# When the extra work of a causal attention is issued: turns and narrow products in steps of their own, queries and keys in VectorE's banks, a shorter first load, the last sends after the attention

## The chip, the cores and the metric

The kernel runs on one core of a Trainium2 chip. The metric is the device time of one execution in microseconds (us). A core has five engines that work side by side, each through a queue of its own: TensorE (PE), VectorE (DVE), ScalarE (ACT), GpSimd (POOL) and SyncE (SP, which here issues most DMAs). Matmul results land in PSUM[...]. The clock at which TensorE runs varies with time, and the profile shows what was granted as a share of full speed.

## The reference

The input x has 16 sequences of 512 rows with 128 channels, float32. Two transformer blocks follow one another, cut here to what matters:

```python
x = x + attn0(layernorm(x)) @ w_proj.T + b_proj   # causal, 16 heads of 8, qkv with bias
x = x + moe(layernorm(x))      # 8 experts 128->512->128, exact gelu, top 2 by softmax
x = x + attn1(layernorm(x))    # not causal, 16 heads of 8, no output projection
x = x + ffn(layernorm(x))      # silu(gate) * up, 352 wide, operands rounded to FP4 blocks
```

The change lies in the first attention and in what runs beside it: the gate of the mixture of experts (logits, the two best experts, the place of each row in its expert's list) and the sending of the normalised rows to those places in DRAM.

## The kernel before, in words

**Groups and steps.** A sequence's 16 heads are taken in four groups (`G = 4`) of two pairs of strips, and a group's keys in four blocks of 128 (`NC = 4`). One *step* is one group with one key block, so a sequence is 16 steps and the first attention 256. The loop at L1015 issues, step by step, what TensorE does: row maxima (`row_max`, tile ps_max) for the group three ahead (`LEAD = 3`), scores (`score`, ps_sc), and the value products of the step before (`attend`, ps_av, put off through the list `behind`). In the first two steps of a group a maximum and a score are each issued in two parts, in the order maximum, score, extra work, maximum, score; in the last two steps there is one of each. In the third step of a group the sums of the group before are turned and divided (`divide`, ps_d, L840).

**How the maxima get into the scores.** After every second group `part_max` splits the maxima in two halves (DVE), `put_max` turns them (ps_mx) and writes them as rows mT into the strips q by DMA (L777), where the next scores need them.

**Extra work.** All else hangs on four dictionaries with a step's number as key. `soon` runs at the head of the step, `ahead` and `later` between the first and the second parts, `last_of` at the end (L1039 to L1059). The extra work of a sequence consists of three lists:

- *The prologue* of a coming sequence b (`prologue`, L639), which starts at position 8 (of 0 to 15) of the sequence two before and takes positions 12 to 17 for its turn, queries, keys, values, spreads and bias: layer norm (`stats`, `moments` with a power on POOL at L203, `scale` with the normalised xn by ACT at L214), the turn of xn (ps_t), the products for queries and keys (`split`, ps_qk, with a rounded half hi by ACT at L656 and the remainder lo by DVE at L669), their writes to DRAM (L678) and DMAs that spread them over the strips, eight and one more for each half (`first` and `second`, L687), the values (ps_v) and the output bias added to x by POOL (`biased`, L713).
- *The end* of a finished sequence: position 3 of the next one turns the result (`turn_back`, aT), position 4 multiplies it by w_proj (`finish`, ps_o).
- *The gate* (`gate_after`, L991), with offsets counted from position 4: norm of the new x (xg by ACT at L214), its turn, the logits (`logits`, ps_g, four matmuls of 8 columns), and in every second sequence `choices`: seven pieces of DVE work, among them the ranks (`place`, ps_n), and then 16 `send`s, one per step, each an indirect DMA issued by POOL (L520). For the last two sequences the gate runs by single sequence and has eight sends. `clear_steps` (L363) fills with zeros what no row will be sent to: `rest`, and eight `region`s, on SP's queue.

**What is in order.** `in_order` (L152) chains every matmul and turn in the order in which the program issues them, and so most of POOL's work. `Lane` (L167) does the same for every DVE instruction of the first attention that goes through `vec`. ACT's order and SP's come from the scheduler, by the program's order and what it estimates. The waits on data are added to this.

**PSUM.** Tiles from `for_dve` take one of two pairs of banks (pool ps_s): ps_max, ps_d, ps_o, ps_g, ps_n, and in general what DVE reads. Tiles from `for_act` take one of four single banks in turn (pool ps_c): ps_sc, ps_av, ps_t, ps_mx, ps_v and, before, ps_qk.

**Start.** L76 to L84 load the constants and all 16 sequences (256 KB each) on SP's queue; bqk's columns `bp` follow (L591). The prologues of sequences 0 and 1 and the maxima of the first three groups run ahead of the loop. `strips` (L618) and `value_columns` (L628) fill the constant parts of the strips and of the values.

**End.** After the loop the remaining sequences are finished, and what is left in `later` is issued in the order of steps (L1075): the gate of the last sequence and its sends, and the plan of the experts' tiles. Then the mixture of experts loads its first tile of rows.

The lines at which the extra work of a step is issued:

```python
if maxima:
    maxima.pop(0)()
scores.pop(0)()
if now in ahead:
    ahead.pop(now)()
...
for f in later.pop(now, []):
    f()
for f in maxima + scores:
    f()
if now in last_of:
    last_of.pop(now)()
```

## Time and profile before

| what | before |
| --- | --- |
| runs, us | 2481.8, 2484.9, 2493.6 (median 2484.9) |
| profiled execution: time of its own, and span | 2462.05, 2460.2 us |
| mean granted clock of TensorE | 0.922 |
| instructions | 38583 |
| start, to the first score of the loop | 0 to 62.7 us |
| first attention, to the end of the loop | 62.7 to 926.3 us |
| one sequence of it, mean of numbers 1 to 13 (least, most) | 54.27 (48.96, 58.92) us |
| first turns of the mixture of experts | 972.3 us |
| second attention, about | 1290 to 2100 us |

Times inside the trace count from the start of the span. The profiled execution is one of its own, and it need not have the time of the runs' median: here it is 22.9 us shorter. In the profile's engine table, the columns are busy time, share of the span and number of instructions; PEld are TensorE's weight loads, which overlap its matmuls. In the slices, each digit is a fortieth of the span in tenths of full load, and PEclk is the granted clock. In the list of stretches, the row gives from and to, the length, the busy time with the number of instructions for PE, PEld, DVE, ACT and POOL, the clock, the mean load of the DMA engines and GB/s. In the timeline, a row gives the start, the length, the engine, line, operation and tiles, how many such instructions, and in brackets what the engine waited for just before. Nearly all matmuls and turns carry the lines of the helpers, L264 and L267, so tiles tell them apart.

### The profile page before, as it was taken

The numbers are of one execution on the slowest core, as the hardware profiler recorded it, in microseconds if no ns is written. First come the engines' busy times: TensorE is split into PE (matmuls) and PEld (weight loads), VectorE is DVE, ScalarE is ACT, GpSimd is POOL, SyncE is SP. The second block draws the span as 40 slices with busy tenths as digits, with TensorE's granted clock in tenths as the row PEclk, the third lists the DMA queues.
The fourth block names the chain that finished last, engine by engine and source line by source line (L and its number), as shares of the span: only waits on it lengthen the run. The fifth ranks groups of instructions, "written<-read, shape, count | busy, mean of one in ns | idle before, by whom it ended". The sixth has DMA issues, their size and how long they took to land.

```text
span 2460.2 us, 38583 instructions
## 1 busy us (share of the span) xinstructions
PE 2138.1 (87%) x13324; PEld 1067.2 (43%) x13324; DVE 1710.3 (70%) x3106; ACT 1389.1 (56%) x2716; POOL 891.4 (36%) x1384
## 2 busy tenths in 40 slices
PE   5999999999999973989998899999899999957776
PEld 2444444444444431656665333333333333335454
DVE  5666666666666636956435788888788888488887
ACT  1565655555565541332334777777777777844443
POOL 4334453545454444032002333322333321054453
PEclk7999998899898975999999999999999999978888
DMA  6112222222122292445552222322232221000000
GB/s 185 54 56 64 62 73 66 88 80 70 60 67 65 62 125 66 140 139 161 158 150 66 63 90 75 85 63 64 63 91 75 83 63 54 2 5 13 18 18 17
DMA packets 156929, 184.47 MB, mean 75 GB/s; under 512 B 25647, under 2 KB 120976, under 8 KB 148544
## 3 DMA queue, kind: packets, MB, share of 16 engines
q1 hardware_dynamic: 147806, 164.55, 23.9%
q0 software_dynamic: 8352, 17.20, 2.5%
q8 instruction: 107, 1.75, 0.3%
q14 instruction: 86, 0.70, 0.1%
q10 hardware_dynamic: 578, 0.26, 0.1%
HBM read 116.55 MB, written 63.28 MB: 73 GB/s over the span
## 4 chain that ended last, share of the span: by engine, by line
PE 38%; DVE 14%; ACT 4%; POOL 3%; issue 2%; DMA 1%; POOLq 0%; ACTq 0%; DVEq 0%
PE ps_av L264 10%; PE ps_max L264 7%; PE ps_h L264 5%; PE ps_sc L264 5%; PE ps_y L264 5%; DVE mx L751 4%; ACT pt L804 3%; PE ps_gu L264 2%; DVE q_t L1123 1%; PE ps_qk L264 1%; DVE q_t L1124 1%; POOL xn L250 1%; DVE q_m L1115 1%; POOL q_v L1112 1%; PE ps_t L267 1%
## 5 line engine op out<-in xcount | busy, mean ns | idle before, releaser
L751 DVE TENSOR_REDUCE mx<-ps_max 128x2 f32<-128x1024 f32 (+1 forms) x896 | 1014.8, 1147 | 385.0 <-PE ps_max L264 373.9
L804 ACT ACTIVATE pt<-ps_sc 128x512 f32<-128x512 f32 (+2 forms) x1792 | 900.8, 568 | 474.7 <-PE ps_sc L264 447.0
L264 PE MATMUL ps_av<-pt,va 128*32 128x512 f32 (+3 forms) x4096 | 498.6, 553 | 19.8 <-POOL pt L809 14.4
L264 PE MATMUL ps_sc<-q,k 64*128 64x512 f32 (+3 forms) x2048 | 461.5, 413 | 30.2 <-ACT pt L804 24.6
L264 PE MATMUL ps_max<-k,q 64*128 64x512 f32 (+3 forms) x2048 | 437.7, 445 | 31.9 <-DVE mx L751 31.5
L809 POOL TENSOR_SCALAR_AFFINE_SELECT pt<-pt 128x128 f32<-128x128 f32 (+1 forms) x768 | 249.6, 332 | 437.2 <-ACT pt L804 421.1
L264 PEld LDWEIGHTS ps_max<-k,q 64*128 64x128 f32 x2048 | 190.2, 193 | 459.3 <-issue 164.4
L264 PEld LDWEIGHTS ps_sc<-q,k 64*128 64x128 f32 x2048 | 220.6, 191 | 161.8 <-ACT pt L804 85.7
L1242 ACT ACTIVATE h<-ps_h,b1t 128x512 f32<-128x512 f32 x156 | 107.1, 687 | 193.6 <-PE ps_h L264 193.5
L264 PE MATMUL ps_y<-w2t,h 128*128 128x128 f32 x1248 | 148.6, 278 | 6.0 <-DVE yt L1256 6.0
L264 PE MATMUL ps_h<-xT,w1t 128*128 128x512 f32 x312 | 150.7, 615 | 3.3 <-DVE xT L275 1.9
L264 PEld LDWEIGHTS ps_av<-pt,va 128*32 128x32 f32 x4096 | 85.7, 110 | 154.2 <-issue 101.2
L264 PEld LDWEIGHTS ps_y<-w2t,h 128*128 128x128 f32 x1248 | 144.4, 194 | 8.6 <-DVE yt L1256 6.4
L1176 POOL DMA_INDIRECT got<-y_rows,backs x128 | 124.1, 970 | 63.0 <-issue 32.5
L520 POOL DMA_INDIRECT x_rows<-xg,slots x128 | 126.2, 986 | 50.8 <-issue 33.5
L264 PE MATMUL ps_max<-mask_bf,ident_bf 128*128 128x128 bf16 (+1 forms) x768 | 130.8, 255 | 0.0
L236 POOL TENSOR_TENSOR ln_rstd<-ln_ve,mhalf 128x4 f32<-128x4 f32 x32 | 34.5, 1079 | 251.2 <-DVE ln_nm L238 248.4
L264 PE MATMUL ps_gu<-wgT,xqT 128*128 128x352 f32 x128 | 67.9, 620 | 63.5 <-DVE hid L1369 35.0
L177 DVE RECIPROCAL rec<-ps_d 128x16 f32<-128x16 f32 x128 | 32.1, 251 | 92.5 <-PE ps_d L267 92.5
L662 POOL TENSOR_TENSOR lo<-full,hi 128x512 fp32r<-128x512 f32 x32 | 41.0, 1282 | 148.3 <-ACT hi L660 148.3
L264 PE MATMUL ps_qk<-xnT,wp 128*128 128x512 f32 x128 | 80.2, 714 | 11.8 <-ACT pt L804 10.4
L835 ACT COPY av_sb<-ps_av 128x512 f32<-128x512 f32 x128 | 75.8, 592 | 16.0 <-PE ps_av L264 11.5
(205 smaller groups left out, 2362.1 us busy)
## 6 DMA issues: line engine op xcount, KB each, us to landing
q<-d SPq DMA_DIRECT2D x256, 128.0 KB
k<-d SPq DMA_DIRECT2D x256, 128.0 KB
d<-hi SPq DMA_DIRECT2D x64, 256.0 KB
d<-lo SPq DMA_DIRECT2D x64, 256.0 KB
xt<-x_rows SPq DMA_DIRECT2D x39, 262.0 KB
w1t<-in_w_dram SPq DMA_DIRECT2D x39, 256.0 KB
w2t<-in_w_dram SPq DMA_DIRECT2D x39, 256.0 KB
y_rows<-yt SPq DMA_DIRECT2D x39, 256.0 KB
```

The costliest lines, as they stand in the source:

```text
L177: ins = f(*args, **kw)
L236: in_order(nc.gpsimd.tensor_tensor(rstd, ve, mhalf, ALU.pow), queue="pool")
L250: ins = (by or nc.gpsimd).tensor_scalar(xn[:, c, 0:E], xb[:, c, :], nm[:, c : c + 1], rstd[:, c : c + 1], ALU.add, ALU.mult,)
L264: return in_order(nc.tensor.matmul(out, lhsT, rhs, start=start, stop=stop))
L520: ins = in_order(nc.gpsimd.indirect_dma_start(out=x_rows[:, :], out_offset=bass.IndirectOffsetOnAxis(ap=slots[:, b0 + u, k, c : c + 1], axis=0
L662: nc.gpsimd.tensor_tensor(lo, full, hi.bitcast(F32), ALU.subtract),
L751: nc.vector.tensor_reduce(hv["mx"][:, c, :, p0 : p0 + m], s4, AX.X, ALU.max),
L804: nc.scalar.activation(pt[:, 0 : m * n], ps[:, 0 : m * n], AF.Exp, scale=SCALE)
L809: nc.gpsimd.affine_select(head, head, pattern=[[0, m], [1, P]], base=0, channel_multiplier=-1, compare_op=ALU.is_ge, fill=0.0,),
L835: nc.scalar.copy(t, acc.pop(0))
L1176: ins = in_order(nc.gpsimd.indirect_dma_start(out=got[:, c, :], out_offset=None, in_=y_rows[0 : min(NT, NE * (b + 1)) * TS, :], in_offset= ...
L1242: nc.scalar.activation(h[:, f, :], ps, AF.Gelu, bias=t["b1"][:, f : f + 1])
```

## The change

It has four parts, all in the first attention; the second attention and everything after are left as they are, and the same instructions are issued, in another order and with other banks.

1. **Steps.** The dictionary `ahead` is no longer used by the first attention. The prologue of sequence b hangs on fixed positions of sequence b - 2: statistics 5 steps before that sequence begins and moments 1 before, xn at its position 3, the bias at 4, its turn at 5, queries and keys together at 7 (their remainders at the end of that step), half of the spreads at 9, the values at 11, the other half 16 steps on. The gate moves too: xg from offset 3 to 4 (position 7 to 8), its turn from 4 to 5 (position 9), the logits in two halves at offsets 6 and 7, the ranks and what follows one step each from offset 8 on.
2. **Banks.** In the first attention, queries and keys share one pair of VectorE's banks in place of two single banks of ScalarE's ring.
3. **Start.** Only two sequences are loaded first; the other 14 loads are issued on SP's queue after the spreads of sequences 0 and 1. The weights' copies move behind the first statistics, and what makes the bias row (a copy, two matmuls, a copy) moves behind the second ones, as `bias_rows`.
4. **End.** The sends of sequence 14 move behind the loop, and the fill `rest` no longer orders the sends.

Offsets in `todo` count from `step`, which is position 4 of the next sequence, and `whens` chooses between the head of the step, its middle and its end. The core of the diff:

```diff
@@ -78,10 +78,13 @@
 
 
     xs = []
-    for b in range(B):
-        xb = cp.tile([P, NC, E], F32, name=f"x{b}")
-        nc.sync.dma_start(out=xb, in_=x_in[b].rearrange("(c p) e -> p c e", p=P))
-        xs.append(xb)
+    xs = [cp.tile([P, NC, E], F32, name=f"x{b}") for b in range(B)]
+
+    def fetch(b):
+        return nc.sync.dma_start(out=xs[b], in_=x_in[b].rearrange("(c p) e -> p c e", p=P))
+
+    for b in range(2):
+        fetch(b)
 
 
     wqkv_sb = cp.tile([E, 3 * E], F32, name="wqkv_sb")
@@ -368,10 +371,11 @@
         def rest():
             vec.tensor_copy(ends_at, free[0:1, :])
             at = NE * CAP + REST
-            nc.sync.dma_start(
+            ins = nc.sync.dma_start(
                 out=rows_of(x_rows, slice(at, at + TS)),
                 in_=zeros.to_broadcast([P, TS // P, ROW]),
             )
+            tc.declare_no_dep(ins.ins, group="sent", reason="other rows")
 
         def region(e):
             at = nc.sync.value_load(
@@ -411,16 +415,22 @@
         def turned(u):
             st["xnT"] = transposed(pool, for_act, st[u], "xnT", nc.scalar.copy)
 
-        def logits(u):
+        def logits(u, part):
             xnT = st["xnT"]
-            if u == 0:
+            if u == 0 and part == 0:
                 st["lg"] = small("g_lg")
-            ps = for_dve("ps_g")[:, 0, 0 : NC * NE]
-            for c in range(NC):
-                mm(ps[:, c * NE : (c + 1) * NE], xnT[:, c * P : (c + 1) * P], wg_sb)
+            if part == 0:
+                st["ps"] = for_dve("ps_g")[:, 0, 0 : NC * NE]
+            for c in range(NC // 2 * part, NC // 2 * (part + 1)):
+                mm(
+                    st["ps"][:, c * NE : (c + 1) * NE], xnT[:, c * P : (c + 1) * P], wg_sb,
+                    start=c == 0, stop=c == NC - 1,
+                )
+
+        def logits_out(u):
             vec.tensor_tensor(
                 st["lg"][:, u * NC : (u + 1) * NC, :],
-                ps.rearrange("p (c e) -> p c e", e=NE),
+                st.pop("ps").rearrange("p (c e) -> p c e", e=NE),
                 bg_bc.to_broadcast([P, NC, NE]),
                 ALU.add,
             )
@@ -511,9 +521,11 @@
                 vec.tensor_copy(to[:, :, E + 2 : E + 3], d[:, at])
                 vec.tensor_copy(to[:, :, E : E + 1], st["r", 1][:, at])
 
+
         choices = [
-            first_of_two, second_of_two, both, place, lambda: (taken(), slot(1)),
-            lambda: (slot(2), shares()), fill,
+            ((0, logits_out), (1, first_of_two)), ((1, second_of_two),), ((1, both),),
+            ((1, place),), ((0, taken), (1, lambda: slot(1))),
+            ((1, lambda: (slot(2), shares())),), ((1, fill),),
         ]
 
         def send(u, k, c):
@@ -531,7 +543,7 @@
             if b0 + u < B - 2:
                 tc.declare_no_dep(ins.ins, group="cleared", reason="other rows")
 
-        return norm, turned, logits, choices, send
+        return norm, turned, logits, logits_out, choices, send
 
 
 
@@ -595,12 +607,14 @@
 
 
...
+            def bias_rows():
...
@@ -647,7 +661,12 @@
                 st["xnT"] = transposed(front, for_act, st["xn"], "xnT", nc.scalar.copy)
 
             def split(t):
-                ps = for_act("ps_qk")
+                if causal:
+                    if t == 0:
+                        st["ps"] = for_dve("ps_qk")
+                    ps = st["ps"][:, t, :]
+                else:
+                    ps = for_act("ps_qk")
                 mm(ps, wp[:, t, :], st["xnT"])
                 hi = front.tile([P, S], F32R, tag="hi", name=f"hi{t}")
                 lo = front.tile([P, S], F32R, tag="lo", name=f"lo{t}")
@@ -684,9 +703,11 @@
                 cols = slice(NHF * hf, NHF * (hf + 1))
                 for dst, parts, order in ((qs[n], st[0], (0, 0, 1, 1)), (ks[n], st[1], (0, 1, 0, 1))):
                     for c in range(4):
-                        nc.sync.dma_start(
+                        ins = nc.sync.dma_start(
                             out=dst[c::D].bitcast(F32), in_=parts[order[c]][:, cols, :]
                         )
+                if b < 2 and causal:
+                    in_order(ins, queue="sp")
                 nc.sync.dma_start(out=qs[n][SM::SM_STEP].bitcast(F32), in_=zrow.rearrange("l o c p -> l o (c p)").to_broadcast([4, NHF, S]))
                 mx = front.tile([P, NC, 2, NHF], F32, tag="mx", name="mx", bufs=3)
                 halves[b, hf] = dict(q=qs[n], k=ks[n], mx=mx)
@@ -716,8 +737,8 @@
 
                 return dict(
                     stats=stats, moments=moments, scale=scaled, turn=turn, biased=biased,
-                    q=lambda: split(0), q_low=lambda: low(0), k=lambda: split(1),
-                    k_low=lambda: low(1), first=lambda: spread(0), values=values,
+                    both=lambda: (split(0), split(1)), low=lambda: (low(0), low(1)),
+                    first=lambda: spread(0), values=values,
                     second=lambda: spread(1),
                 )
             return norm, turn, lambda: split(0), lambda: split(1), lambda: spread(0), values, (
@@ -909,36 +930,53 @@
         soon, later, last_of = {}, {}, {}
         ahead = {}
         if causal:
-            weights_turned()
-            pattern()
-            pro = [prologue(0), prologue(1)]
+            pro = {b: prologue(b) for b in range(3)}
 
             def run(b, *names):
                 for name in names:
                     pro[b][name]()
 
             run(0, "stats", "moments")
+            weights_turned()
+            pattern()
             strips(0)
-            run(0, "scale", "turn", "q", "q_low", "k", "k_low", "first")
             run(1, "stats", "moments")
+            bias_rows()
+            run(0, "scale", "turn", "both", "low", "first")
             value_columns(0)
-            run(0, "values", "biased")
+            run(0, "values")
             strips(1)
             run(0, "second")
-            run(1, "scale", "turn", "q", "q_low", "k", "k_low")
+            run(1, "scale", "turn", "both", "low")
+            run(0, "biased")
             strips(2)
             run(1, "first")
             value_columns(1)
             run(1, "values", "biased")
             strips(3)
             run(1, "second")
+            for b in range(2, B):
+                in_order(fetch(b), queue="sp")
             for n in range(LEAD):
                 for fs in max_steps(n):
                     for f in fs:
                         f()
                 if n == 2:
                     value_columns(2)
+                    run(2, "stats", "moments")
                 max_done(n)
+            for b in range(2, B):
+                if b not in pro:
+                    pro[b] = prologue(b)
+                T = NC * G * (b - 2)
+                for name, at, when in (
+                    ("stats", -5, last_of), ("moments", -1, last_of), ("scale", 3, later),
+                    ("biased", 4, later), ("turn", 5, later), ("both", 7, later),
+                    ("low", 7, last_of), ("first", 9, later), ("values", 11, later),
+                    ("second", 16, later),
+                ):
+                    if T + at >= 0:
+                        when.setdefault(T + at, []).append(pro[b][name])
         else:
             for b in range(2, B):
                 later.setdefault(NC * (G * b - 6) - 8, []).append(lambda b=b: collect(front, b))
@@ -995,41 +1033,51 @@
             u = b % ng
             if u == 0:
                 gate[0] = gate_steps(pool, for_act, for_dve, b, ng)
-            norm, turned, logits, choices, send = gate[0]
+            norm, turned, logits, logits_out, choices, send = gate[0]
             stats, moments, scale = norm(u)
-            todo = [
-                (1, stats), (2, moments), (3, scale), (4, lambda: turned(u)), (5, lambda: logits(u))
-            ]
+            whens = soon, later, last_of
+            todo = [(1, 2, stats)]
+            if ng == 2:
+                todo += [
+                    (2, 2, moments), (4, 1, scale), (5, 1, lambda: turned(u)),
+                    (6, 1, lambda: logits(u, 0)), (7, 2, lambda: logits(u, 1)),
+                ]
+                if u == 0:
+                    todo.append((8, 0, lambda: logits_out(u)))
+                turns = [8 + m for m in range(len(choices))]
+            else:
+                todo += [
+                    (2, 1, moments), (3, 1, scale), (5, 1, lambda: turned(u)),
+                    (6, 1, lambda: logits(u, 0)), (6, 2, lambda: logits(u, 1)),
+                ]
+                turns = [7, 8, 8, 9, 10, 10, 11]
             if u == ng - 1:
                 rows = [(v, k, c) for v in range(ng) for k in range(2) for c in range(NC)]
-                todo += [(5 + m // (3 - ng), f) for m, f in enumerate(choices)]
-                start = 5 + len(choices) // (3 - ng)
+                for d, fs in zip(turns, choices):
+                    todo += [(d, w, lambda f=f: f(u) if f is logits_out else f()) for w, f in fs]
+                start = turns[-1] + 1
                 if b == B - 1:
-                    todo.append((start, lambda: plan_tiles(pool)))
-                todo += [(start + 1 + m, lambda r=r: send(*r)) for m, r in enumerate(rows)]
+                    todo.append((start, 2, lambda: plan_tiles(pool)))
+                if b == B - 2:
+
+                    start = NC * len(groups) + 3 - step
+                todo += [
+                    (start + (m if ng == 2 else 0), 1, lambda r=r: send(*r))
+                    for m, r in enumerate(rows)
+                ]
                 if b == B - 3:
-                    todo += [(start + 1 + m, f) for m, f in enumerate(clear_steps())]
-            for d, f in todo:
-                later.setdefault(step + d, []).append(f)
+                    todo += [(turns[5] + m, 1, f) for m, f in enumerate(clear_steps())]
+            for d, w, f in todo:
+                whens[w].setdefault(step + d, []).append(f)
 
         for n, (b, g) in enumerate(groups):
             nxt = n + LEAD
-            if nxt % G == 1 and nxt // G + 1 < B:
...
+            if not causal and nxt % G == 1 and nxt // G + 1 < B:
+                ...
             steps = max_steps(nxt)
             score, attend, leave = main_parts(b, g)
             for kc in range(NC):
@@ -1055,8 +1103,8 @@
                     f()
                 for f in maxima + scores:
                     f()
-                if now in last_of:
-                    last_of.pop(now)()
+                for f in last_of.pop(now, []):
+                    f()
 
                 while behind:
                     behind.pop(0)()
```

## The prediction

> **What bounds the kernel now.** I read the page's engine table and slices first, then busy time by stretch (one stretch per sequence of the first attention), then the list of waits, then the timeline around the steps that the change touches.
>
> ```profile
> PE 2138.1 (87%) x13324; PEld 1067.2 (43%) x13324; DVE 1710.3 (70%) x3106; ACT 1389.1 (56%) x2716; POOL 891.4 (36%) x1384
> ...
> PE   5999999999999973989998899999899999957776
> ...
> PEclk7999998899898975999999999999999999978888
> ```
>
> TensorE is the busy engine, and in slices 7 to 14, inside the first attention, its granted clock is below full. By sequence (from, to, and then us, busy time with counts of PE, PEld, DVE, ACT, POOL, clock, DMA share, GB/s):
>
> ```profile
> 266.60:324.88 58.28, 55.56 (x379) 26.15 (x377) 37.43 (x90) 31.71 (x69) 19.89 (x52) 0.85 0.21 65
> 324.88:375.87 50.99, 48.53 (x370) 23.60 (x368) 33.27 (x60) 31.29 (x68) 33.56 (x66) 1.00 0.24 77
> ...
> 864.64:926.27 61.63, 43.44 (x255) 19.34 (x253) 15.77 (x60) 26.58 (x58) 29.97 (x63) 0.74 0.93 125
> ```
>
> Sequences 4 and 5 do nearly the same matmuls; the one at clock 0.85 takes 7.3 us longer. The last one is 61.63 us with a third less matmul work: it has waits of its own. Sequences 1 to 13 (110.68 to 816.18) average 54.27 us.
>
> Starts of the first score matmul of four consecutive steps without extra work:
>
> ```profile
> 375.87 0.50 PE L264 MATMUL ps_sc<-q,k 64*128 64x512 f32 x2
> ...
> 378.48 0.44 PE L264 MATMUL ps_sc<-q,k 64*128 64x384 f32 x2
> ...
> 381.41 0.50 PE L264 MATMUL ps_sc<-q,k 64*128 64x256 f32 x4
> ...
> 383.90 0.44 PE L264 MATMUL ps_sc<-q,k 64*128 64x128 f32 x4
> ```
>
> So such steps take 2.61, 2.93 and 2.49 us (the last with its four ps_d turns), and a plain fourth one 1.59: 9.62 a group, 38.5 for the 16 steps of a sequence. The rest is extra work and stalls. The stalls near the end of sequence 4:
>
> ```profile
> 316.23 1.13 PE L264 MATMUL ps_qk<-xnT,wp 128*128 128x512 f32 x2 [0.74 <-ACT pt L804]
> ...
> 320.25 0.43 PE L264 MATMUL ps_sc<-q,k 64*128 64x128 f32 x3 [0.73 <-DVE lo L177]
> ...
> 321.11 2.08 PE L264 MATMUL ps_v<-wqkv_sb,xnT 128*128 128x128 f32 x8 [0.43 <-ACT pt L804]
> ```
>
> ps_qk and ps_v wait for a bank of ScalarE's ring; both halves of q and k sit in that ring too. And step 8 of sequence 4's successor:
>
> ```profile
> 347.43 0.36 DVE L177 SCALAR_TENSOR_TENSOR ln_nm<-ln_mv,ln_rstd 128x4 f32<-128x4 f32 x1 [1.11 <-POOL ln_rstd L203]
> ...
> 347.83 1.65 ACT L214 ACTIVATE xg<-x,ln_nm,ln_rstd 128x128 f32<-128x128 f32 x4 [1.11 <-DVE ln_nm L177]
> ...
> 348.37 1.48 PE L267 MATMUL ps_t<-cst,xg 128*128 128x128 f32 x4 [0.76 <-ACT xg L214]
> ...
> 349.38 1.06 ACT L804 ACTIVATE pt<-ps_sc 128x512 f32<-128x512 f32 x2
> ```
>
> The turn of xg takes 1.48 + 0.76 us where an unhindered one takes 0.6, and the exponentials of the same step queue on ACT behind xg. At the end of the stage:
>
> ```profile
> 880.52 0.98 POOL L520 DMA_INDIRECT x_rows<-xg,slots  x1 [8.17 <-DMA x_rows<-zeros]
> ...
> 923.28 0.96 POOL L520 DMA_INDIRECT x_rows<-xg,slots  x1 [8.77 <-DMA x_rows<-zeros]
> ```
>
> POOL's sends wait for zero fills, the causal selects queue behind them, and ps_av waits 14.0 us in two waits (5.3 and 8.7).
>
> [...] eight ps_av matmuls of 512 columns take 1.07 us in one place and 1.90 at 312.40, in a half-clock stretch. [...] scores ready at 347.6 had their exponentials at 349.38, behind xg. [...]
>
> **The change, part by part.** Instruction counts on every engine are unchanged; order and banks move. The built order of the changed program is the second source below.
>
> *1. Spreading the extra work (sequences 1 to 13).* PE time of it at full clock, from the timeline: turn of at 0.59, output product 0.99, two turns of maxima 2 x 0.54, two turns of rows 2 x 0.60, q and k 2 x 1.03, narrow gate products 0.99, v 1.09, ranks 0.34 in every second sequence. Sum 8.1; with 38.5, a floor of 46.6 against 54.27. The change sets one turn at step 5, q and k at 7, a turn at 9, half of the gate products at 10 and at 11, v at 11, ranks at 15. What goes:
> - bank waits of ps_qk (10.4 us in 14 waits), ps_v (7.1) and ps_sc behind lo (4.7): q and k now take one pair of VectorE's two pairs of banks, and v's bank is freed by an exponential of the step before;
> - the ranks' single-pair stretch: today ps_n holds one pair from 303.56 to 309.19 and row maxima take turns with DVE; later ps_n is read before the next maximum needs its pair;
> - half-clock stretches begun by these stalls.
>
> What comes, worked out from the same durations:
> - *Step 3 to 4.* xn (1.65) now stands before the copy of aT on ACT. Exponentials end 1.16 us into step 3, xn 2.80, aT 3.4; the output product could start at 2.6. Wait 0.85.
> - *Step 7 to 8.* Count from the first score of step 7. qk0 ends at 1.43, qk1 at 2.5; hi 1.55 to 2.24 and 2.6 to 3.3; lo (0.74) ends at 3.05 and 4.1. The next maximum stands before ln_nm on DVE: its reduction (1.22) runs 4.1 to 5.33, ln_nm to 5.5. On ACT xg stands ahead of step 8's own exponentials in every such sequence: 5.55 to 7.2, the first exponential to 7.75. PE has done two maxima, the first scores and one more by 5.1; its next score needs the bank that this exponential frees. Wait 2.75. The pair of q and k is free at 4.1, wanted at 4.25: no wait, by a thin margin.
> - [...] I charge one half-clock window after it: 3.4 us that do the work of 1.7, part of it idle anyway, 1.5. Bounds: 0 and 6 (below).
> - Small ring waits 0.3.
>
> 46.6 + 0.85 + 2.75 + 1.5 + 0.3 = 52.0, or 2.3 less than 54.27: 13 x 2.3 = 30 us. Sequences 0 and 14, without this gate or this prologue, lose some stalls: -2. DVE's, POOL's and SP's moved work (statistics, bias, 8 spreads of 0.6 us each at step 9 and 8 at step 16 in place of 16 at 16) lies beside PE: they are busy 65%, 50% and less, and the maxima that they load are wanted four steps later.
>
> *2. Sends and fills.* The fill called rest no longer orders sends, and the eight sends of sequence 14 leave POOL's queue until after the last selects: both ps_av waits go, -14.0. The eight then run between sequence 15's ln_rstd (939.07) and its first send (950.57): 8 x 1.26 = 10.1 of 11.5 us, hidden. If the fills land late, they push the rest. Bounds -14 and 0.
>
> *3. The start.* The load of bp no longer stands behind 16 loads, so hi comes at 17 instead of 20.21; but ln_nm now stands behind the bias copies and xn starts at 12.8 as before. Spreads begin some 1.6 us earlier, and the strip fills (4.16 us at 35.21) no longer stand just ahead of the first reductions: the maxima end some 5.6 us earlier. Against that, 14 loads (3.67 MB, 12.7 us at the 290 GB/s of 5 to 15 us) now stand on SP between the last spread (about 48) and the first mT rows; these land at about 64, and the first score, at 62.70 now, needs them: +1. Bounds -6 and +6.
>
> Sum: -30 - 2 - 14 + 1 = **-45 us**. The profiled execution is 2462.05 us (span 2460.2), 22.9 below the median of the runs, 2484.9; the difference is taken from the median: **2440**. From the last placement on, each engine's order is as before, so I expect nothing in later stages. Half a per cent, 12.4 us, is about what a measurement of this kernel tells from no change.
>
> **Rivals.**
> - *No block at step 8* (15%): if xg were early enough, each sequence takes 47.4: 13 x 6.9 = 89 instead of 30, **2381**. For: clock 1.00 and few stalls in sequences 1, 5, 13. Against: ACT's order.
> - *The gain goes to the clock* (10%, no change): sequences 3 and 9 spend 12.9 us on steps 8 and 9, where sequence 5 spends 8.8; a stall followed by three half-clock windows costs 4.1 instead of 1.5: 30 shrinks to -4, **2474**.
> - *Slower by the same place* (10%): the block at step 8 keeps the clock at half until step 12. It decides from a clock loss of 4.8 us a sequence (54.27 - 50.5 + 15/13, part 2 and 3 giving 15); at 6.0 it is 13 x 1.2 = 16 slower, **2501**. For: POOL's sends and three half-clock windows in sequences 3 and 9. Against: none of 13 sequences shows four after step 8.
> - *The start eats the change*: +6 instead of +1 alone changes little; inside the range.
>
> **How the numbers follow.** The main case has 65%, 2415 to 2465 by the bounds of its terms. Adding most of the first rival and of the second gives 2378 to 2480, leaving out the slow one and the tails. Faster: 0.65 + 0.15 = 0.80; same 0.10; slower 0.10.
>
> **What would show it.** Right: ps_qk and ps_v without waits on ACT; a PE wait of some 2.7 us at step 8 ended by an exponential that stands behind xg, and a clock dip after it; sequences of 51 to 53 us; no DMA wait in POOL's sends before the last select; first score near 64. Wrong: sequences near 47 or 55 us, or a new ring wait at steps 9 or 11, or a shorter time won outside the first attention.

## The result, and the profile after

| | before | changed |
| --- | --- | --- |
| median of the runs, us | 2483.35 (2478.92 to 2493.6) | 2516.55 (2510.72 to 2520.48) |
| ratio | | 1.0126, 95% interval 1.0088 to 1.0164 |
| profiled execution: time of its own, and span, us | 2462.05, 2460.2 | 2510.72, 2509.0 |
| one sequence, mean of numbers 1 to 13, us | 54.27 | 57.27 |
| start of sequence 15 to the first ps_h of the mixture of experts, us | 110.8 | 93.9 |

The change made the kernel slower by 1.3%, some 31 us. A gain of 45 us had been forecast.

The page of the changed kernel, engine table and slices (lines of the code have moved: L264, L267, L804, L177, L214 and L656 of before are L267, L270, L825, L180, L217 and L675 here):

```profile
PE 2167.2 (86%) x13324; PEld 1077.6 (43%) x13324; DVE 1703.2 (68%) x3106; ACT 1388.2 (55%) x2716; POOL 886.1 (35%) x1384
...
PE   6998999999999983989998898999889999957776
...
PEclk8999898799999785999999999999999999978888
```

The number of matmuls is the same and their busy time has grown, from 2138.1 to 2167.2 us. Without new work it grows where the clock is lower (a score took 0.50 us at full clock and 0.79 at half, below): the two slices with a 7 ahead of the middle, at 439 to 502 and 815 to 878 us, hold the ends of sequences 6 and 13.

Sequences 5 and 6 of the changed kernel, and the stretch from sequence 15 to the first ps_h in it and in the kernel before (columns as in the list of stretches; the last line is of before):

```profile
331.95:386.63 54.68, 50.22 (x371) 24.12 (x370) 34.40 (x76) 31.48 (x68) 30.25 (x64) 0.94 0.24 75
386.63:453.96 67.33, 63.20 (x381) 30.09 (x379) 35.32 (x76) 31.93 (x69) 23.97 (x58) 0.73 0.19 58
...
904.77:998.70 93.93, 47.38 (x314) 24.60 (x312) 48.11 (x168) 30.95 (x68) 57.65 (x89) 0.69 0.68 103
...
864.64:975.40 110.76, 55.34 (x313) 27.10 (x311) 44.46 (x158) 30.85 (x68) 57.56 (x89) 0.63 0.58 90
```

The two sequences hold nearly the same work; at clock 0.73 it took 12.7 us longer. The stretch at the end is 16.8 us shorter than before, where 14 had been forecast. The two ps_av waits of 14.0 us went, as forecast, but a new wait stands in the last sequence:

```profile
PE ps_sc L267 <- DMA q<-mT: 7.5, 1, 7.5
```

TensorE's waits in sequences 1 to 13 (us in total, times, longest):

```profile
PE ps_sc L267 <- ACT pt L825: 28.7, 13, 2.2
PE ps_qk L267 <- ACT hi L675: 10.1, 13, 0.8
PE ps_max L267 <- DVE lo L180: 7.4, 13, 0.6
PE ps_o L267 <- ACT aT L278: 7.3, 13, 0.6
```

The old waits of ps_qk and ps_v for exponentials are gone, as forecast. Four others stand in their place, once in each of the 13 sequences: 0.57 us at step 4 (ps_o), 0.78 at step 7 (ps_qk), 0.57 (ps_max) and 2.21 (ps_sc) at step 8.

The timeline of steps 7 and 8 in sequence 3, TensorE:

```profile
242.34 1.12 PE L267 MATMUL ps_qk<-xnT,wp 128*128 128x512 f32 x2
244.24 1.12 PE L267 MATMUL ps_qk<-xnT,wp 128*128 128x512 f32 x2 [0.78 <-ACT hi L675]
...
247.59 0.50 PE L267 MATMUL ps_max<-k,q 64*128 64x512 f32 x2 [0.57 <-DVE lo L180]
...
250.95 0.79 PE L267 MATMUL ps_sc<-q,k 64*128 64x512 f32 x1 [2.21 <-ACT pt L825]
```

and VectorE and ScalarE in the same steps:

```profile
246.13 1.41 DVE L180 SCALAR_TENSOR_TENSOR lo<-ps_qk,bp,hi 128x512 fp32r<-128x512 f32 x2 [3.36 <-ACT hi L675]
247.45 1.22 DVE L772 TENSOR_REDUCE mx<-ps_max 128x2 f32<-128x1024 f32 x1
248.58 0.16 DVE L180 SCALAR_TENSOR_TENSOR ln_nm<-ln_mv,ln_rstd 128x4 f32<-128x4 f32 x1
...
248.77 1.65 ACT L217 ACTIVATE xg<-x,ln_nm,ln_rstd 128x128 f32<-128x128 f32 x4 [2.68 <-DVE ln_nm L180]
250.33 2.05 ACT L825 ACTIVATE pt<-ps_sc 128x512 f32<-128x512 f32 x4
```

Read backwards it is the forecast chain: the score at 250.95 needs a bank that an exponential frees, the exponentials queue behind xg, xg waits for ln_nm, and ln_nm stands behind lo and a reduction. In front of it stands a link that I had not seen: the second ps_qk waits for hi, which reads the first one. And the score that ends the wait takes 0.79 us where the one before it took 0.50: the clock has fallen to half. It does so during or just after this wait in each of the 13 sequences, and nowhere else in them: for 6.8 us eight times, 10.2 us three times, and 44.4 and 34.1 us in sequences 6 and 13. By the clock that the traces record that is 163.8 us at half clock, against 109.2 in the kernel before.

**What the two profiles cannot tell.** Their spans differ by 48.8 us, more than the runs. 26.4 us of that lie in the second attention, which took 824.6 us before and 851.0 after (from the start of its first ps_av, at 1330 us in the kernel before, to that of its last, at 2155), with the same instructions in the same order on every engine. It is not the change: below, the kernels that ran together on one chip all had 824 to 826 us, or all 849 to 852, whatever their code. The kernel before itself had medians of 2448.64 and 2450.84 us on the two chips of the first kind and 2477.09 on the one of the second. Its profile was of the first kind. If the runs behind its median of 2484.9 were of the second, that would also account for the 22.9 us between the two; the record does not show it.

### The profile page after: what moved, and what is told of

The parts are those of the page before. It is cut to its first block, busy times and chain, and to the rows that moved or that the text cites. A ratio compares the mean times of both kernels' runs of the same rounds, so it can differ in the third digit from the quotient of the medians.

```text
span 2509.0 us, 38679 instructions
## 1 busy us (share of the span) xinstructions
PE 2167.2 (86%) x13324; PEld 1077.6 (43%) x13324; DVE 1703.2 (68%) x3106; ACT 1388.2 (55%) x2716; POOL 886.1 (35%) x1384
## 4 chain that ended last, share of the span: by engine, by line
PE 65%; DVE 19%; ACT 7%; POOL 4%; issue 3%; DMA 2%; SPq 1%; POOLq 0%; ACTq 0%; DVEq 0%
PE ps_av L267 17%; PE ps_max L267 15%; PE ps_sc L267 11%; DVE mx L772 7%; PE ps_h L267 4%; PE ps_y L267 4%; ACT pt L825 3%; PE ps_qk L267 3%; PE ps_gu L267 2%; PE ps_t L270 2%; PE ps_d L270 2%; PE ps_v L267 1%; DVE q_t L1172 1%; PE ps_mx L270 1%; PE ps_o L267 1%
## 5 line engine op out<-in xcount | busy, mean ns | idle before, releaser
L825 ACT ACTIVATE pt<-ps_sc 128x512 f32<-128x512 f32 (+2 forms) x1792 | 900.3, 569 | 479.1 <-PE ps_sc L267 454.9
L267 PE MATMUL ps_sc<-q,k 64*128 64x512 f32 (+3 forms) x2048 | 485.1, 422 | 78.3 <-ACT pt L825 57.5
L267 PE MATMUL ps_av<-pt,va 128*32 128x512 f32 (+3 forms) x4096 | 503.8, 560 | 4.6 <-ACT pt L825 1.1
L267 PE MATMUL ps_max<-k,q 64*128 64x512 f32 (+3 forms) x2048 | 446.3, 453 | 33.5 <-DVE mx L772 24.5
L267 PEld LDWEIGHTS ps_max<-k,q 64*128 64x128 f32 x2048 | 193.5, 196 | 469.1 <-issue 200.8
L267 PEld LDWEIGHTS ps_sc<-q,k 64*128 64x128 f32 x2048 | 229.6, 195 | 223.8 <-ACT pt L825 121.3
L267 PE MATMUL ps_h<-xT,w1t 128*128 128x512 f32 x312 | 151.3, 617 | 3.4 <-DVE xT L278 1.8
L267 PE MATMUL ps_y<-w2t,h 128*128 128x128 f32 x1248 | 148.7, 278 | 6.3 <-DVE yt L1305 6.3
L267 PEld LDWEIGHTS ps_av<-pt,va 128*32 128x32 f32 x4096 | 85.6, 111 | 146.1 <-issue 94.7
L267 PEld LDWEIGHTS ps_y<-w2t,h 128*128 128x128 f32 x1248 | 144.5, 194 | 8.9 <-DVE yt L1305 6.7
L267 PE MATMUL ps_max<-mask_bf,ident_bf 128*128 128x128 bf16 (+1 forms) x768 | 133.5, 260 | 0.0
L267 PE MATMUL ps_gu<-wgT,xqT 128*128 128x352 f32 x128 | 67.0, 613 | 62.0 <-DVE hid L1418 33.2
L267 PE MATMUL ps_qk<-xnT,wp 128*128 128x512 f32 x128 | 75.8, 675 | 13.8 <-ACT hi L675 12.5
L270 PE MATMUL ps_d<-cst,av_sb 128*128 128x128 f32 x512 | 85.6, 291 | 1.4 <-ACT av_sb L856 1.4
L267 PEld LDWEIGHTS ps_h<-xT,w1t 128*128 128x128 f32 x312 | 51.2, 192 | 77.8 <-ACT h L1291 53.3
```

What stands on the lines that cost most here:

```text
L267: return in_order(nc.tensor.matmul(out, lhsT, rhs, start=start, stop=stop))
L270: return in_order(nc.tensor.transpose(out, src, ident))
L825: nc.scalar.activation(pt[:, 0 : m * n], ps[:, 0 : m * n], AF.Exp, scale=SCALE)
```

## The experiments

Each ratio is to the kernel before, run on the same chip; the changed kernel is at 1.0126 and, in a second measurement, 1.016. Times of a sequence are means of numbers 1 to 13 in the one execution that was profiled. Two executions of the same code differed by 1.2 us a sequence with half-clock stretches (57.27 and 58.45, the changed kernel) and by 0.08 without (49.80 and 49.72, early ln_nm). Of each edit the core is shown; lines have moved again, so go by tiles.

**xg behind the exponentials.** ScalarE's order is written out (`in_order` with a queue of its own for hi, xg and the exponentials), and xg is issued at the end of step 8:

```diff
...
-                    (2, 2, moments), (4, 1, scale), (5, 1, lambda: turned(u)),
+                    (2, 2, moments), (4, 2, scale), (5, 1, lambda: turned(u)),
```

> The changed kernel, with ScalarE's order written out so that xg stands behind all four exponentials of step 8 instead of ahead of them; the turn of xg stays at step 9. Theory 1 (the block at step 8, and the half-clock windows that its idle time starts, cost the time): the wait of ps_sc on an exponential at step 8 (2.2 us, changed kernel) falls under 0.5 us, the turn of xg at step 9 waits 0.5 to 1.5 us instead, no half-clock stretch of 6.8 us or more begins at step 8, sequences 1 to 13 take 49 to 52 us instead of 57.3 on average, and the whole 2425 to 2450 us against 2516. Theory 2 (the clock falls for another reason, such as the thinner mix of work at steps 8 to 11): only the wait goes, 13 x 2.2 = 29 us, 2488, and the half-clock stretches stay.

Ratio 0.9901 (0.9871 to 0.9931), a sequence 52.84 us, half clock 61.4 us. The wait of 2.2 us is gone and step 8 takes 3.10 us instead of 6.51. Somewhat less was won than theory 1 said (49 to 52 us a sequence), because the turn of xg at step 9 now runs as slowly as xg comes:

```profile
245.02 1.63 PE L272 MATMUL ps_t<-cst,xg 128*128 128x128 f32 x4 [0.39 <-ACT xg L217]
```

It takes 1.63 us instead of the 0.66 of an unhindered turn, and half-clock stretches, most of them of 3.4 or 6.8 us, begin there in 9 of 13 sequences.

**ln_nm early.** The same written order, with ln_nm in the middle of step 7 and xg right behind hi:

```diff
...
-                    (2, 2, moments), (4, 1, scale), (5, 1, lambda: turned(u)),
+                    (2, 2, moments), (3, 1, scale.shift), (3, 2, scale), (5, 1, lambda: turned(u)),
```

> The changed kernel with ln_nm of the gate issued in the middle of step 7, ahead of lo on VectorE, so that xg on ScalarE starts right behind hi and not at 5.55 us; ScalarE's order is that of the changed kernel. Theory 1: the wait at step 8 shrinks from 2.2 to about 0.7 us, too short to start a half-clock stretch; sequences 1 to 13 take 49.5 to 51.5 us, the whole about 2425 to 2440. Theory 2: only 1.5 us a sequence, 2496.

Ratio 0.9727 (0.9687 to 0.9768), a sequence 49.80 us, no half-clock stretch in sequences 1 to 13. Its timeline at the same place, sequence 3:

```profile
232.97 0.36 DVE L180 SCALAR_TENSOR_TENSOR ln_nm<-ln_mv,ln_rstd 128x4 f32<-128x4 f32 x1 [1.11 <-POOL ln_rstd L206]
...
235.08 1.64 ACT L222 ACTIVATE xg<-x,ln_nm,ln_rstd 128x128 f32<-128x128 f32 x4
...
236.62 1.06 ACT L833 ACTIVATE pt<-ps_sc 128x512 f32<-128x512 f32 x2
236.68 0.50 PE L275 MATMUL ps_max<-k,q 64*128 64x512 f32 x2 [0.57 <-DVE lo L180]
237.11 0.28 PE L275 MATMUL ps_max<-mask_bf,ident_bf 128*128 128x128 bf16 x2
237.33 0.51 PE L275 MATMUL ps_sc<-q,k 64*128 64x512 f32 x2
```

Both scores run at full clock without a wait. The edit also writes ScalarE's order out, but that changed nothing: by the traces, the order of TensorE, ScalarE and POOL in sequences 1 to 13 is that of the changed kernel, and on VectorE ln_nm alone stands elsewhere. So one instruction of 0.36 us, moved ahead of lo, takes 3.9% off the changed kernel (0.9727 over 1.0126, each to before on its own chip): this is theory 1, and theory 2 (1.5 us a sequence) is out.

**Filling the idle time.** The block stays, and TensorE adds its mask again and again in place of waiting:

```diff
...
-                    mm(s4[:, j, :, n - P : n], ident_bf, mask_bf[:, 0:m, :], start=False)
+                    for k in range(1 + extra):
+                        mm(s4[:, j, :, n - P : n], ident_bf, mask_bf[:, 0:m, :], start=False, stop=k == extra)
```

> The changed kernel with the idle time of step 8 filled: the second maximum of that step, in sequences 1 to 13, adds its mask ten times instead of once (18 more 128-column bf16 matmuls, about 2.0 us at full clock; masked scores only get more negative). The block on ScalarE stays as it is. Theory 1 in its second half (the idle time starts the half-clock windows): step 8 keeps its length to within 1 us, but the half-clock stretches of 6.8 to 44 us after it are gone, which is worth 3.5 us in a plain sequence and 10 to 12 in numbers 6 and 13: about 60 us, 2455. If the stretches come from the mix of work and not from this idle time, they stay and the time is 2516 or a few us more.

Ratio 1.0013 (0.9982 to 1.0044), a sequence 55.33 us, half clock 95.6 us. The stretches were not gone, as had been expected. The fill was too short: it took 1.0 us, half of the 2.0 expected, and left 1.21 idle, and 7 of 13 sequences still had a stretch, two of them of 30.7 and 41.0 us. Hence a second, with 20 masks more a bank:

> As the fill before, with 20 more masks a bank instead of 9 (the 9 took 1.0 us and left 1.2 of the 2.2 us idle, after which 7 of 13 sequences still had a half-clock stretch). Theory: with less than 0.3 us idle left, step 8 still takes 5.2 to 6 us as ScalarE's order has not changed, but no sequence has a half-clock stretch at steps 8 to 15; they take 51 to 52.5 us, and the whole is 1.5 to 2.5% below the changed kernel. If the dense mask products of 64 or 128 columns do not count as activity, the stretches stay.

Ratio 0.989 (0.986 to 0.9921), 2.7% below the changed kernel on the same chip. No half-clock stretch is left in sequences 1 to 13:

```profile
242.31 2.52 PE L267 MATMUL ps_max<-mask_bf,ident_bf 128*128 128x128 bf16 x42
244.76 0.99 PE L267 MATMUL ps_sc<-q,k 64*128 64x512 f32 x2
```

Step 8 still takes 5.81 us, but a sequence only 52.43. The changed kernel needs 58.45 on that chip and 57.27 in its first profile. With the block left as it is, the clock alone costs 4.8 to 6.0 us a sequence, more than the four waits together (4.1).

**The end alone**, on the kernel before: `rest` without an order to the sends, and

```diff
...
+                if b == B - 2:
+                    at = NC * len(groups) + 3 - step
+                    todo += [(at, lambda r=r: send(*r)) for r in rows]
...
```

> The kernel before with the fourth part of the change alone: the sends of sequence 14 behind the loop, the fill called rest without an order to the sends. Theory: both ps_av waits (5.3 and 8.7 us) go, and sequence 15 falls from 61.6 to about 44 to 48 us; a wait of the scores on the rows mT behind the fills takes some of it (7.5 us in the changed kernel). 2466 to 2472 against 2483. Rival: the wait only moves, to the mT rows or to the first tile of the mixture of experts, and the whole stays within 5 us of 2483.

Ratio 0.9952 (0.9934 to 0.997), 12 us. From the start of sequence 15 to the first ps_h it took 92.4 us in place of 110.8. The ps_av waits for POOL's selects went, and a wait of 3.6 us on the rows mT came:

```profile
PE ps_sc L264 <- DMA q<-mT: 3.6, 1, 3.6
```

The 18.4 us of the stretch are from two single executions; the runs say 12, and they decide. Sequences 1 to 13, whose code is that of before, took 53.44 us in this profile and 54.27 in that of before, so much of the kernel before varies between executions by itself.

**The changed kernel again:**

> The changed kernel once more, on the chip of the first experiments. In its first profile the second attention took 851 us; in the profiles of the kernel before and of four variants it took 824 to 826, with the same order on every engine. If those 26 us belong to that execution and not to the change, it takes 824 to 826 us here, and the ratio to the kernel before is again about 1.01, as part 1's loss (3.0 us in each of 13 sequences, 39) less the gain of the end (about 18) leaves 20 us or 0.8%. If the change causes them, it takes about 851 us.

Ratio 1.016 (1.0114 to 1.0207), a sequence 58.45 us: this execution had three stretches of 34 to 44 us instead of two. It ran on another chip than the first experiments, though meant for theirs. The second attention took 852.2 us, and so did not come back to 825 as the first alternative asked. But the three other kernels run with it took 849.4, 850.5 and 848.6, and those run at other times 823.6 to 825.7. The two fills, which differ in one number, had 823.6 and 850.5. It goes with where and when a kernel ran, not with the kernel; what sets it, no run here shows.

**Queries and keys back in ScalarE's ring**, all else as changed:

```diff
...
-                if causal:
-                    if t == 0:
-                        st["ps"] = for_dve("ps_qk")
-                    ps = st["ps"][:, t, :]
-                else:
-                    ps = for_act("ps_qk")
+                ps = for_act("ps_qk")
```

> The changed kernel with its second part undone: queries and keys in single banks of ScalarE's ring, at step 7 as in the changed kernel. Theory 1 (the block is ScalarE's order, not the banks): the waits on hi (0.78) and lo (0.57) before the maxima go, the scores wait for lo and for the exponentials instead, the idle time at step 8 stays over 2 us and the half-clock stretch with it; within 0.7% of the changed kernel. Rival (the pair taken from the maxima makes the block): the idle time falls under 1 us, and the kernel gains 1.5% or more on the changed one.

Ratio 1.0033 (1.0012 to 1.0054), 1.3% below the changed kernel on that chip, so outside the 0.7% of theory 1 and short of the 1.5% of the rival. A sequence takes 54.55 us. The waits on hi and lo went and the idle time at step 8 stayed:

```profile
PE ps_sc L267 <- ACT pt L820: 33.3, 14, 2.4
```

Half clock follows it in all 13 sequences. The pair of banks does not make the block, but it costs about 1.05 us at step 7 (4.55 against 3.50).

**Two more waits out of the version with early ln_nm**: both ps_qk ahead of hi, and xn behind the copy of aT:

```diff
...
+                        for v in range(2):
+                            mm(st["ps"][:, v, :], wp[:, v, :], st["xnT"])
...
-                    ("stats", -5, last_of), ("moments", -1, last_of), ("scale", 3, later),
+                    ("stats", -5, last_of), ("moments", -1, last_of), ("scale", 3, last_of),
```

> The kernel with the early ln_nm, and two more waits of the changed kernel taken out: both products of queries and keys issued ahead of hi (0.78 us at step 7), and xn behind the copy of aT on ScalarE (0.57 us at step 4). Theory: 1.2 to 1.4 us a sequence less than the kernel with early ln_nm alone (49.8), so 48.4 to 48.6, 16 to 18 us in the whole: about 0.966 of the kernel before. If hi, now later by 1 us at step 7, delays lo and the maxima of step 8, half of it comes back as a wait there.

Ratio 0.9772 (0.9745 to 0.98), a sequence 50.59 us: a miss, slower than 49.80. Step 4 fell to 3.99 and step 7 to 3.50 us, but with hi later, lo came later, and the maximum of step 8 waited twice as long as before:

```profile
PE ps_max L275 <- DVE lo L180: 14.9, 13, 1.1
```

After 1.1 us of idle time instead of 0.57, 9 of 13 sequences had a half-clock stretch of 6.8 us. The wait did not only move; it grew, and half clock came with it.

**Early ln_nm, xn behind aT, and the choice of banks**, three kernels on one chip. With the ring:

> The kernel with early ln_nm, with xn behind the copy of aT on ScalarE, and with queries and keys in single banks of ScalarE's ring. Theory: against the kernel with early ln_nm alone (49.8 us a sequence), the waits of 0.57 (ps_o), 0.78 (second ps_qk) and 0.57 us (maximum behind lo) go: 47.9 to 48.5 us, 20 to 25 us less in the whole; no half-clock stretch in sequences 1 to 13. If the ring's banks, held until lo has ended, stop the scores of step 8, a wait of 0.5 us or more on lo or on an exponential stands there and a part of the sequences has a half-clock stretch.

With the pair of banks:

> As the last, with queries and keys left in VectorE's pair of banks: only the wait of 0.57 us before ps_o goes. 49.2 us a sequence, 7 us less than the kernel with early ln_nm alone, and 13 us more than the version with the ring.

And the early ln_nm alone:

> The kernel with early ln_nm once more, on the chip of the two versions above, so that the three can be compared. 49.8 us a sequence and no half-clock stretch, as before; its ratio to the kernel before 0.97.

| version | ratio to before (95%) | median, us | a sequence, us | half clock, us |
| --- | --- | --- | --- | --- |
| ring | 0.9602 (0.9574 to 0.963) | 2352.87 | 47.98 | 0 |
| pair | 0.967 (0.9643 to 0.9696) | 2370.45 | 49.12 | 0 |
| early ln_nm alone | 0.9712 (0.9684 to 0.974) | 2380.4 | 49.72 | 0 |

Each step is worth about what the removed waits say: 0.60 us a sequence for aT (a wait of 0.57), 1.14 for the banks (0.78 and 0.57). The version with the ring beats both kernels, by 4.0% the one before. Its sequence 3, at full clock:

```profile
203.53:251.11 47.58, 46.84 (x370) 23.31 (x368) 34.91 (x75) 31.25 (x68) 30.25 (x63) 1.00 0.28 86
```

## Why the prediction was wrong

The experiments give each term of a sequence's sum by a difference of two versions:

| term, us a sequence | forecast | measured | as the difference of |
| --- | --- | --- | --- |
| floor 46.6 and small ring waits 0.3 | 46.9 | 47.98 | version with the ring |
| aT behind xn, step 4 | 0.85 | 0.60 | early ln_nm alone, less the pair |
| q and k in one pair, steps 7 and 8 | 0 | 1.14 | the pair, less the ring |
| block at step 8 | 2.75 | 2.71 | longer fill, less early ln_nm alone |
| half clock | 1.5 | 4.84 | changed kernel, less the longer fill |
| sum | 52.0 | 57.27 | |

- **The clock is the step that failed.** I charged one half-clock window, 1.5 us a sequence, with bounds of 0 and 6; that there would be one was my estimate. Half clock cost 4.84, and 6.02 in the second profile of the changed kernel. No sequence had one window: each had at least two, and in sequences 6 and 13 half clock lasted 44.4 and 34.1 us, over the end of the one and nearly to that of the other. This is 3.3 of the 5.3 us by which the sum was short.
- **The other 1.9 us** were short without the clock: 50.5 was forecast and the longer fill took 52.43. "No wait, by a thin margin" for the pair of q and k was wrong: the second product waits 0.78 us for hi to have read the first half of the shared pair, and the next maximum 0.57 for lo, which began only after the second hi. The floor, whose extra work adds to 8.2 us and not to 8.1, was 1.1 us too low with its ring waits; even the version with the ring keeps some idle time (in its sequence 3, TensorE is busy 46.84 of 47.58 us).
- **Step 7 to 8** was traced rightly in its main link: a wait of 2.75 us on an exponential behind xg was forecast, 2.21 stood there, and the block cost 2.71.
- **The whole.** 57.27 instead of 52.0 us is 13 x 5.3 = 69 us, and 2440 becomes 2509; the median was 2516.55. The 2 us from sequences 0 and 14 did not come: they took 47.37 and 49.18 us after 47.99 and 48.46.
- **Where the bound went.** The rival on the slower side named this place and 2501 us. Its threshold is 4.9 us a sequence by its own terms, not 4.8, and the clock loss of 4.84 alone would have left the time as it was; with the other 1.9 us it became slower. I gave it 10% because no sequence of the kernel before showed four half-clock windows after step 8. That was no evidence: there TensorE's waits for xg were about 0.8 us, a third of the wait to come. What spoke for it, four half-clock windows in a row from the end of sequence 6 on, was in the same trace.
- **"The gain goes to the clock"** put the loss at 4.1 us a sequence and so at no change. It rested on the clock, as the result does, with 4.1 where 4.84 was measured, and took the other terms as forecast.
- **No block at step 8** was priced at 47.4 us a sequence (without the 0.3 of ring waits) and 2381. Two of the experiments are this rival: 49.80 with one instruction moved, 47.98 with the other waits gone too.
- **Sends and fills**, -14: 12 us by itself, and from sequence 15 to the first ps_h 16.8 us less. The waits of 14.0 us went, but 7.5 us came back on the rows mT; the busy time of TensorE in the stretch fell too, from 55.34 to 47.38 us for one matmul more, at clock 0.69 instead of 0.63: these 7.96 us are about what the new wait took. That the number came out right is in part luck.
- **The start**, +1: the first score came at 63.88 against 62.70 us. Over all profiles it came between 61.9 and 64.6 with the new start, and at 62.70 and 64.70 with the old, so that 1 us of it cannot be told from nothing; the start was not tried alone. In the changed kernel the rows mT were issued from 59.66 us on, behind the 14 loads (48.34 to 59.55); that they would also land behind them was my assumption, which no run tests.
- **Nothing in later stages** was right, though the profiles alone would have said otherwise.

## What to carry to other kernels

Price a wait of TensorE in two parts: its length, and the work that may then run at half clock. In this kernel a block with a 2.2 us wait cost 2.7 us by itself and 4.8 to 6.0 us more after it. At step 8 a longest wait of 0.57 us was followed by half clock in 0 of 13 sequences, one of 1.1 or 1.21 us in 9 and 7 of 13; but look also at what TensorE does around the wait (next section). Before spreading work over more steps, walk through the order on the engine that frees the banks, and find the small instruction (here ln_nm) on which a long one in that queue waits. When two profiles differ in a stage that the change does not touch, look at that stage in other kernels run at the same time before explaining it.

## What the runs showed of the hardware

How often a half-clock stretch follows step 8 in sequences 1 to 13, by the longest wait there:

| longest wait, us | kernel | sequences with a stretch |
| --- | --- | --- |
| 0.57 | early ln_nm; fill of 2.5 us | 0 of 13, in each |
| 1.1 | both ps_qk ahead of hi | 9 of 13 |
| 1.21 | fill of 1.0 us | 7 of 13 |
| 2.2 | changed kernel | 13 of 13, twice |
| 2.4 | queries and keys in the ring | 13 of 13 |

I had not expected waits so short to make a difference. But the longest wait does not account for all of it. With xg behind the exponentials it is 0.39 us, and 9 of 13 sequences have a stretch after the slow turn of 1.63 us. In the kernel before, 5 of the 16 stretches in sequences 1 to 13 begin after 3.41 us without any idle time of TensorE. What follows are counts from the profiles of the kernel before and of the changed one, in sequences 1 to 13; they tell what went together there, and no run varied one of these things alone.

In both profiles the clock's records begin at the marks of a grid of 3.41 us, to within 3 ns, and all half-clock stretches are multiples of it, from 3.4 to 44.4 us. Here are two pairs of neighbours on this grid, in sequences 2 and 4 of the kernel before (columns as in the list of stretches):

```profile
184.42:187.83 3.41, 3.41 (x28) 1.87 (x26) 2.65 (x9) 2.43 (x6) 1.37 (x5) 1.00 0.00 0
187.83:191.25 3.42, 3.42 (x34) 1.78 (x30) 3.25 (x13) 1.15 (x3) 2.18 (x5) 1.00 0.00 0
290.24:293.66 3.42, 3.42 (x30) 2.20 (x30) 2.74 (x5) 2.73 (x6) 1.46 (x5) 1.00 0.00 0
293.66:297.07 3.41, 3.41 (x16) 0.90 (x16) 2.08 (x10) 0.87 (x2) 1.59 (x3) 0.50 0.00 0
```

The first of each pair is busy throughout and holds 1.06 us of the narrow products ps_g. It holds 0.91 us of ps_av in sequence 2, where full clock goes on, and 0.42 in sequence 4, where half clock follows. The kernel before has 10 stretches of the grid (windows) at full clock that are busy for all their 3.41 us and hold 1.06 us of ps_g: half clock followed the 5 with 0.42 or 0.43 us of ps_av and none of the 5 with 0.90 to 1.06. So busy time alone does not tell the two kinds apart. The changed kernel issues ps_g in two halves and has no such window. By busy time, half clock followed all 13 windows at full clock with less than 2.1 us (all 13 in the changed kernel, with 1.15 to 1.91), 11 of the 71 between, and only those 5 of the 259 with 2.95 us or more.

Nor had I expected that half clock, once there, can outlast a stage in which TensorE is hardly idle. In the stretch of 44.4 us it was busy for 43.96. The busy time of ps_av alone there, in windows of 3.4 us, with the clock behind it (from, to, us, busy time of PE, PEld and ACT, clock, DMA share, GB/s), was

```profile
417.10:420.50 3.40, 0.65 (x8) 0.20 (x8) 0.58 (x1) 0.53 0.82 224
...
447.80:451.20 3.40, 1.50 (x8) 0.20 (x8) 0.00 (x0) 0.50 0.01 2
...
458.10:461.50 3.40, 1.67 (x8) 0.20 (x8) 0.00 (x0) 0.50 0.19 58
461.50:464.90 3.40, 1.12 (x12) 0.16 (x8) 0.00 (x0) 0.97 0.00 0
```

The window with the most ps_av work is the last one at half clock, and full clock follows it. In the two profiles 80 windows of the grid are at half clock. All 19 with more than 1.6 us of ps_av were the last of their stretch, 8 of the 17 between, and of the 44 with less than 1.0 us only 2. Why ps_av goes with the end of half clock stays open. Its matmuls stand in the timeline as `128*32`, a score's or a maximum's as `64*128`, but a first number of 128 does not tell it, for the turns (ps_t, ps_d) are `128*128`, and of the 12 half-clock windows with 0.9 us or more of them only 1 was the last.
